# Two attention layers of a graph network run as one loop of units

## The chip, the core and the metric

The kernel runs on one core of one Trainium2 chip. The metric is the device time of one execution in microseconds. A core has TensorE (PE, matmuls; its weight loads are shown as PEld), VectorE (DVE), ScalarE (ACT), GpSimd (POOL, which issues the gathers here) and SyncE (SP, which issues the plain transfers). Each engine works through its own queue in order; semaphores tie the queues together.

## What is computed

Four graph layers follow each other on 3327 nodes with 512 features: a graph attention (layer 0), a neighbourhood mean with linear maps (layer 1, the "sage" stage), and two more attentions (layers 2 and 3). Each takes `h = relu(layernorm(x))` and adds its result to `x`. The two layers that the change touches have one form:

```python
hp = jnp.einsum('nd,hdf->hnf', h, W)              # 8 heads of 64 features
f_src = jnp.einsum('hnf,hf->hn', hp, a_src)
f_dst = jnp.einsum('hnf,hf->hn', hp, a_dst)
e = jax.nn.leaky_relu(f_src[:, :, None] + f_dst[:, None, :], ALPHA)
e = jnp.where(adj[None] > 0, e, NEG_FILL)
att = jax.nn.softmax(e, axis=-1)
out = jnp.einsum('hij,hjf->hif', att, hp)
out = jax.nn.elu(jnp.transpose(out, (1, 0, 2)).reshape(N, H * F))
```

The graph is sparse, and its nodes are sorted so that the first ones have far more neighbours than the last.

## The kernel before

Nodes are padded to 3328: 26 blocks of 128 rows, or 52 groups of 64 target nodes. An attention reads a table in HBM with one row of 528 words for each source node: eight heads of 64 features of `h W`, each with an exponential beside it, and eight more exponentials. `PLAN` gives each group three counts: dense blocks (128 table rows that lie together, brought by SP), mixed and pure rows sets (128 table rows each, picked by an index list and gathered by POOL). Group 0 has (14, 5, 4), group 1 (6, 4, 6), the last ones about (1, 1, 3). There are 77 dense blocks and 291 gathers in one attention.

Blocks are taken in the order 0, 24, 1, 23, 2, 22, ..., 11, 13, 12, 25 (`ls.order`), each with its two groups. `Lists.units` cuts a group's rows into units: dense and mixed ones in units of up to 2 (`SLOTS`), then pure ones in units of up to 3 (`UNIT`).

`attend` runs over the units; PE, DVE and ACT keep the order in which it is written there. A dense or mixed unit costs VectorE two operations, `mx` (L1553, a maximum of the group's row `r_bc` and the table's exponentials) and `wgt` (L1557, times the mask), and TensorE 32 small matmuls into the group's sum `facc` (L1588). An edge unit (pure rows) costs TensorE a pick `r_of` (L1487), VectorE a sum `w_of` (L1495), a maximum (L1540) and a product `vw` (L1543), and TensorE matmuls into `facc` (L1577). The pick for a unit stands two units ahead in TensorE's order. The row `r_bc` of a group is fetched by SP (`r_two`, L1343) and spread over the partitions by a matmul (L1351). Rows are loaded three units ahead (`AHEAD`), by `take` (L1309 on SP, L1314 on POOL).

At the end of a unit `later` moves everything that runs beside: the endings of groups (`ending`: `sums`, reciprocal, eight scalings into `fhp`, L1404; then `elu_into`, `fin_e` and `fin_x`), and one tick of the next layer's projection. In attention 2 that is `Following` for layer 3. For each finished block of `x3` it normalises (`norm`, on ScalarE), transposes (`p_ps`, L961), forms `p_sd` (L969) and `p_wh` (L980, eight matmul passes of 512 columns for `h W`), scales it into the table row on ScalarE (L989), writes the row to table 3 (L990) and the other values to `r_dram`. One step of it is done in each tick, for at most two blocks, the second starting five ticks after the first (`lag`). When the units of attention 2 are used up, `hurry` hands the projection spare PSUM banks and it goes on with normalisation (`norm_by_columns`, L879 to L888) and scaling (L984) on VectorE. Only when it has ended does the second call of `attend` begin, for attention 3.

The call that the change replaces, and the loop at the end of `attend`:

```python
over.append(True)
if beside is not None:
    mx = aps.tile([P, SLOTS, BANK], F32, name="mx", tag="mx", bufs=1)
    rb = aps.tile([P, BANK], F32, name="r_bc", tag="r_bc", bufs=1)
    beside.hurry((mx[:, 0, :], mx[:, 1, :], rb))
while ends or (beside is not None and beside.busy()):
    later()
```

Of the kernel before, what the change touches and what calls it, by code (L numbers as in the profile page):

```python
# [39 lines left out]
P = 128  # L40
H = 8
# [31 lines left out]
AHEAD = 3  # L73
EPARTS = 5
# [465 lines left out]
class Lists:  # L540
# [46 lines left out]
    def units(self, g):  # L587

        dense, mixed, pure = PLAN[g]
        rows, out = self.rows(g), []  # L590
        for edge, part, most in ((False, rows[: dense + mixed], SLOTS), (True, rows[dense + mixed :], UNIT)):
            n, at = -(-len(part) // most), 0
            for b in range(n):
                w = len(part) // n + (b < len(part) % n)
                out.append((edge, part[at : at + w], self.edge[g] + at))
                at += w
        return out
# [209 lines left out]

class Following:
# [3 lines left out]
    def __init__(self, tc, cs, N, wl, W, WA, table, r_dram, r3, pool, psum, pb, lag, ab=None):  # L812

        self.__dict__.update(locals())
        nc = tc.nc
        if ab is not None:
            self.ab = pool.tile([P, 2, D], F32, name=f"ab{wl}")
            for k, a in enumerate(ab):
                nc.sync.dma_start(self.ab[:, k, :], a.partition_broadcast(P))
        self.NB = table.shape[0] // P  # L820
        self.Wt = pool.tile([P, KC, D], F32, name=f"fWt{wl}")
        nc.sync.dma_start(self.Wt, W.rearrange("(kc p) o -> p kc o", p=P))
        self.hs = pool.tile([P, self.NB, KC], F32, name=f"hs{wl}")
        self.early, self.ready, self.spare, self.taken, self.gone = [], [], None, {}, []

    def begin(self, c, xt):
        self.early.append((self.norm_by_columns if self.spare is not None or self.ab is not None else self.norm)(c, xt))
# [4 lines left out]
    def hurry(self, spare):  # L832

        self.spare = spare

    def bank(self, shape, name, k):
        if self.spare is not None:
            return self.spare[k][: shape[0], : shape[1]]
        return self.psum.tile(shape, F32, name=name, tag="p_ps", bufs=self.pb)

    def tick(self):
        if self.spare is not None:
            for g in self.ready[:2]:
                if next(g) is None:
                    self.ready.remove(g)
            self.step()
            return
        if self.lag:
            for n, g in enumerate(self.ready[:2]):
                if n and self.taken[id(self.ready[0])] < self.lag:  # L850
                    break
                self.taken[id(g)] = self.taken.get(id(g), 0) + 1
                if next(g) is None:
                    self.gone.append(g)
            while self.gone:
                g = self.gone.pop()
                self.ready.remove(g)
                del self.taken[id(g)]
            self.step()
            return  # L860
# [96 lines left out]
    def rest(self, c, hx):  # L957
# [9 lines left out]
        sd = self.bank([P, BANK], "p_sd", 0)  # L967
# [10 lines left out]
        wh = self.bank([P, D], "p_wh", 1)  # L978
        for kc in range(KC):
            nc.tensor.matmul(wh, hT[:, kc, :], self.Wt[:, kc, :], start=(kc == 0), stop=(kc == KC - 1))  # L980
        yield True
        nc.vector.tensor_scalar(sf, sf, -SMALL, SMALL, ALU.max, ALU.min)
        if self.spare is not None:
            nc.vector.tensor_tensor(  # L984
                V[:, :, 0:F], wh.rearrange("p (h f) -> p h f", f=F), V[:, :, F : F + 1].to_broadcast([P, H, F]), ALU.mult
            )
        else:
            for h in range(H):
                nc.scalar.mul(V[:, h, 0:F], wh[:, h * F : (h + 1) * F], V[:, h, F : F + 1])  # L989
        nc.sync.dma_start(self.table[c * P : (c + 1) * P, :ROW], row.bitcast(I32))  # L990
        rs = halves(nc, pp, self.cs, sf, self.r3[:, c, :])
        if self.spare is None:
            yield True
        yield True
        rs, last = rs()
        if self.spare is None:
            yield True
        yield True
        tr = self.bank([2 * H, P], "p_tr", 2)
# [277 lines left out]
def sparse(ctx: ExitStack, tc: tile.TileContext, t: dict, out: bass.AP, WA, ls, cs, idx, rdeg, first):  # L1277
# [41 lines left out]
    def attend(layer, table, r_dram, r3, finish, tick=lambda: None, home=None, beside=None, edges=None):  # L1319
# [5 lines left out]
        width = table.shape[1]  # L1325
        groups = [b * PG + u for b in ls.order for u in range(PG)]
        units = []
        for j, g in enumerate(groups):
            mine = ls.units(g)
            spread_at = sum(not e for e, _, _ in mine) - 1  # L1330
            units += [(j, g, e, rows, s0, i == 0, i == len(mine) - 1, i == spread_at) for i, (e, rows, s0) in enumerate(mine)]
        hq = H // PG
        sw = hq * (F + 1)
        with tc.tile_pool(name=f"fatt{layer}", bufs=2) as ap, tc.tile_pool(
# [5 lines left out]
            def fetch(j):  # L1340
                if j < len(groups):
                    rr = ap.tile([2, H * GB], F32, name="r_two", tag="r_two", bufs=2)
                    nc.sync.dma_start(rr, r_dram[groups[j], :, :, :].rearrange("t h i -> t (h i)"))  # L1343
                    rrs[j] = rr

            def spread(j):


                if j < len(groups):
# [4 lines left out]
            def ending(g, hps={}, made={}):  # L1354

                b, u = divmod(g, PG)
                o0 = u * GB
                fin = finish(b, lambda: hps.pop(b), ap)

                def place():  # L1360

                    if b not in hps and home is None:
                        hp_ = hps[b] = ap.tile([P, D], F32, name="fhp", tag="hp", bufs=3)
                    elif b not in hps:
                        hps[b] = home[:, b, :]
                    return hps[b]
# [4 lines left out]
                if over:  # L1371
                    sm = accs.pop(g)[:, :sw].rearrange("p (q x) -> p q x", x=F + 1)
# [11 lines left out]
                    made[b] = made.get(b, 0) + 1  # L1384
                    if u == PG - 1:
                        while made[b] < PG:
# [4 lines left out]
                nc.scalar.copy(sm, accs.pop(g)[:, :sw])  # L1391
                sm = sm.rearrange("p (q x) -> p q x", x=F + 1)
                yield
                if layer == 2:
# [10 lines left out]
                made[b] = made.get(b, 0) + 1  # L1405
# [4 lines left out]
            def later():  # L1410
# [3 lines left out]
                tick()  # L1414

            def load(i):

                if i < len(units):
                    _, _, e, rows, _, _, _, _ = units[i]
                    if e:  # L1420
                        gi = ap.tile([P, UNIT, width], I32, name="rows_e", tag="rows_e", bufs=5 if layer == 0 else 6)
                    else:
                        gi = ap.tile([P, SLOTS, width], I32, name="rows_s", tag="rows_s", bufs=4 if layer == 0 else 5)
                    loaded[i] = gi
                    take(gi, table, rows)

            def bits(i):

                if layer == 0 and i < len(units):
                    _, g, _, rows, _, _, _, _ = units[i]  # L1430
# [10 lines left out]
            def masks(i, on):  # L1441

                if i < len(units):
                    _, _, e, rows, _, _, _, _ = units[i]
# [12 lines left out]
            def turned(i):  # L1457

                if layer == 0 and i < len(units) and units[i][2]:
                    _, g, _, rows, _, _, _, _ = units[i]  # L1460
# [6 lines left out]
            def kept(i):  # L1467

                if layer == 0 and i < len(units) and units[i][2]:
                    _, g, _, rows, s0, _, _, _ = units[i]  # L1470
# [7 lines left out]
            def pick(i):  # L1478

                if i < len(units) and units[i][2]:  # L1480
                    _, g, _, rows, s0, _, _, _ = units[i]
# [4 lines left out]
                    for k in range(len(rows)):  # L1486
                        nc.tensor.matmul(re[:, k, :], st[:, k, :], r3[mine, b, :], start=True, stop=True)  # L1487

            def summed(i):

                if i < len(units) and units[i][2]:
                    n, re = len(units[i][3]), found.pop(i)
# [3 lines left out]

            for j in range(2):
# [4 lines left out]
            lead = [(ahead + 1 if layer == 0 else 2) if u[2] else 1 for u in units]  # L1502
# [29 lines left out]
            for i, (j, g, e, rows, s0, begins, stops, last_slots) in enumerate(units):  # L1532
                n, m0 = len(rows), rows[0][0]
                gt = loaded.pop(i).bitcast(F32)
# [24 lines left out]
                early(i)  # L1559
                if begins:  # L1560
                    fetch(j + 2)
                    acc = aps.tile([P, BANK], F32, name="facc", tag="acc")
                    accs[g] = acc
# [6 lines left out]
                for k in range(n):  # L1570
# [3 lines left out]
                    if e:  # L1574
                        by = vw[:, k].rearrange("p (q v) x -> p v q x", v=PG)
                        for v in range(PG):
                            nc.tensor.matmul(  # L1577
                                accs[g][v * GB : (v + 1) * GB, :sw].rearrange("p (q x) -> p q x", x=F + 1),
# [6 lines left out]
                    for q in range(hq):  # L1585
                        for v in range(PG):
                            h = q * PG + v
                            nc.tensor.matmul(  # L1588
                                accs[g][v * GB : (v + 1) * GB, q * (F + 1) : (q + 1) * (F + 1)],
# [10 lines left out]
                later()  # L1600
                if stops:
                    ends.append(ending(g))
            over.append(True)
            if beside is not None:
                mx = aps.tile([P, SLOTS, BANK], F32, name="mx", tag="mx", bufs=1)
                rb = aps.tile([P, BANK], F32, name="r_bc", tag="r_bc", bufs=1)
                beside.hurry((mx[:, 0, :], mx[:, 1, :], rb))
            while ends or (beside is not None and beside.busy()):
# [37 lines left out]
    with ExitStack() as mx:  # L1646
# [85 lines left out]
        with tc.tile_pool(name="beside_ps", bufs=1, space=PSUM) as wps:  # L1732
# [8 lines left out]
            attend(0, *first, done, lambda: next(bg, None), y)  # L1741
# [135 lines left out]
    with ExitStack() as l3:  # L1877
        at2 = proj
        proj = following(l3, 3, 2, t["L3_gnn_W"], 2, 5)
        attend(2, at2.table, at2.r_dram, at2.r3, elu_into(x2, x3, proj.begin), proj.tick, beside=proj, edges=edges)  # L1880
    attend(3, proj.table, proj.r_dram, proj.r3, elu_into(x3, out), edges=edges)
# [101 lines left out]
```

## Time and profile before

| what | value |
|---|---|
| median of 3 timed runs | 2659.47 us (2657.05 to 2659.57) |
| the profiled execution | 2389.36 us, its span 2387.6 us |
| mean TensorE clock granted in it | 0.87 |
| busy over the span: PE, DVE, ACT, POOL | 1868.2, 1706.4, 1110.2, 1162.9 us |
| gathers `rows_e`, `rows_s` of the three attentions | 654 and 219, 957 and 964 ns each |
| `p_wh`, `fhp` scalings | from 3.70 us a block, 334 ns each |

Stages by the trace, in us from the start of the span: lists and first projection to about 352, attention 0 to about 860, sage and the projection of layer 2 to 1394, attention 2 to about 1910, the end of its endings and of the projection of layer 3 to 1944, attention 3 to the end. The profiled execution is 270 us shorter than the timed ones; durations below are those of the profiled one. Busy times of PE are modelled, since matmuls overlap.

### The profile page before, as it was taken

The numbers are of one execution on the slowest core, as the hardware profiler recorded it, in microseconds if no ns is written. First come the engines' busy times: TensorE is split into PE (matmuls) and PEld (weight loads), VectorE is DVE, ScalarE is ACT, GpSimd is POOL, SyncE is SP. The second block draws the span as 40 slices with busy tenths as digits, with TensorE's granted clock in tenths as the row PEclk, the third lists the DMA queues.
The fourth block names the chain that finished last, engine by engine and source line by source line (L and its number), as shares of the span: only waits on it lengthen the run. The fifth ranks groups of instructions, "written<-read, shape, count | busy, mean of one in ns | idle before, by whom it ended". The sixth has DMA issues, their size and how long they took to land. (4 is left out here: it accounts for less than half of the span.)

```text
span 2387.6 us, 43165 instructions
## 1 busy us (share of the span) xinstructions
PE 1868.2 (78%) x14899; PEld 1042.4 (44%) x14899; DVE 1706.4 (71%) x3061; ACT 1110.2 (47%) x4149; POOL 1162.9 (49%) x1227
## 2 busy tenths in 40 slices
PE   5888416897888869899999936888888857776875
PEld 4554204454555424333333324555444435444442
DVE  5455866788989895044445549878787749999996
ACT  3566101455666633133333312577796822445543
POOL 1000013476777500477776435655655335776762
PEclk9887757899999979999999968888898966779777
DMA  6676118798889665689888688877787548888883
GB/s 274 245 291 225 42 39 299 264 316 287 270 261 295 197 247 189 216 280 307 292 287 296 219 248 272 246 246 227 235 253 223 155 182 260 271 278 259 278 287 118
DMA packets 213728, 577.63 MB, mean 242 GB/s; under 512 B 37838, under 2 KB 44076, under 8 KB 210174
## 3 DMA queue, kind: packets, MB, share of 16 engines
q0 software_dynamic: 93504, 328.25, 43.6%
q1 hardware_dynamic: 119998, 246.53, 29.8%
q8 instruction: 121, 1.98, 0.3%
q14 instruction: 105, 0.86, 0.1%
HBM read 511.41 MB, written 63.25 MB: 241 GB/s over the span
## 5 line engine op out<-in xcount | busy, mean ns | idle before, releaser
L1314 POOL DMA_INDIRECT rows_e<-table,idx x654 | 625.9, 957 | 363.0 <-issue 148.3
L1577 PE MATMUL facc<-vw,ones_of 128*64 128x260 f32 x2616 | 447.2, 457 | 78.5 <-DVE vw L1543 61.0
L1588 PE MATMUL facc<-rows_s,wgt 128*64 128x65 f32 x7200 | 343.9, 247 | 170.8 <-DVE wgt L1557 115.8
L1588 PEld LDWEIGHTS facc<-rows_s,wgt 128*64 128x64 f32 x7200 | 289.8, 156 | 291.2 <-DVE wgt L1557 147.7
L1543 DVE TENSOR_TENSOR vw<-rows_e,w_of 128x1040 f32<-128x1040 f32 (+1 forms) x270 | 395.6, 1465 | 9.6 <-DVE w_of L1540 0.2
L1314 POOL DMA_INDIRECT z_rows<-h_dram,idx x291 | 278.8, 958 | 237.0 <-issue 156.3
L1314 POOL DMA_INDIRECT rows_s<-table,idx x219 | 211.1, 964 | 239.1 <-PE facc L1588 142.9
L1553 DVE TENSOR_TENSOR mx<-r_bc,rows_s 128x1024 f32<-128x1024 f32 (+1 forms) x255 | 280.4, 1100 | 46.6 <-DMA rows_s<-table 34.1
L1557 DVE TENSOR_TENSOR wgt<-mx,mask 128x1024 f32<-128x1024 f32 (+1 forms) x255 | 280.3, 1099 | 38.4 <-ACT mask L1455 20.9
L1404 ACT ACTIVATE fhp<-sums,rd 64x64 f32<-64x64 f32 x816 | 215.6, 334 | 185.3 <-DVE rd L1397 182.1
L1577 PEld LDWEIGHTS facc<-vw,ones_of 128*64 128x64 f32 x2616 | 195.4, 156 | 225.7 <-issue 94.2
L1867 PE MATMUL sage_acc<-z_rows,z_mask 128*64 128x512 f32 x736 | 188.7, 611 | 11.5 <-DMA z_rows<-h_dram 5.9
L1218 POOL DMA_DIRECT2D list_b<-shift x8 | 4.0, 513 | 325.3 <-DVE shift L1179 325.3
L1820 DVE TENSOR_TENSOR s_o<-n_ps,bn_y 128x512 f32<-128x512 f32 x26 | 18.0, 692 | 150.2 <-PE n_ps L1815 141.8
L1851 ACT CAST z_mask<-mask 128x128 f32<-128x128 uint8 (+1 forms) x201 | 52.5, 284 | 154.4 <-PE sage_acc L1867 154.0
L741 PE MATMUL wh_ps<-fWt,hT 128*128 128x512 f32 x208 | 121.5, 738 | 0.0
L1391 ACT COPY sums<-facc 128x260 f32<-128x260 f32 x153 | 56.1, 367 | 140.5 <-PE facc L1577 139.3
L1404 ACT ACTIVATE bn_y<-sums,rd 64x64 f32<-64x64 f32 x408 | 107.7, 334 | 2.9 <-DVE rd L1397 1.3
L1495 DVE TENSOR_REDUCE w_of<-r_of 128x16 f32<-128x48 f32 (+1 forms) x270 | 61.4, 227 | 62.1 <-PE r_of L1487 35.9
L1867 PEld LDWEIGHTS sage_acc<-z_rows,z_mask 128*64 128x64 f32 x736 | 51.4, 137 | 114.8 <-issue 94.0
L1789 PE MATMUL s_ps<-fWx,hT 128*128 128x512 f32 x208 | 93.9, 605 | 5.1 <-ACT hT L1786 5.1
L1455 ACT ACTIVATE mask<-on 128x128 uint8<-128x128 uint16 (+1 forms) x85 | 25.2, 297 | 153.3 <-DVE on L1433 151.0
(260 smaller groups left out, 3006.8 us busy)
## 6 DMA issues: line engine op xcount, KB each, us to landing
adj_i<-in_adj SPq DMA_DIRECT2D x26, 1664.0 KB
rows_s<-table SPq DMA_DIRECT2D x46, 528.0 KB
table<-v_row SPq DMA_DIRECT2D x78, 264.0 KB
rows_s<-table SPq DMA_DIRECT2D x62, 264.0 KB
rows_s<-table SPq DMA_DIRECT2D x23, 632.0 KB
fin_x<-fx SPq DMA_DIRECT2D x52, 256.0 KB
z_rows<-h_dram SPq DMA_DIRECT2D x23, 512.0 KB
rows_e<-table,idx POOLq DMA_INDIRECT x654
```

The source lines that it names most:

```text
L741: nc.tensor.matmul(wh, hT[:, kc, :], self.Wt[:, kc, :], start=(kc == 0), stop=(kc == KC - 1))
L1314: nc.gpsimd.indirect_dma_start(out=dst, out_offset=None, in_=src[:, :], in_offset=bass.IndirectOffsetOnAxis(ap=idx[:, k : k + 1], axis=0))
L1391: nc.scalar.copy(sm, accs.pop(g)[:, :sw])
L1404: nc.scalar.mul(hp[o0 : o0 + GB, h * F : (h + 1) * F], sm[mine, q, 0:F], rd[mine, q, :])
L1495: nc.vector.tensor_reduce(w[:, :n], re[:, :n].rearrange("p k (t h) -> p k h t", h=H), AX.X, ALU.add)
L1543: nc.vector.tensor_tensor(vw[:, :n], gt[:, :n, : H * (F + 1)].rearrange("p k (h x) -> p k h x", x=F + 1), w[:, :n].unsqueeze(3).to_broadca ...
L1553: nc.vector.tensor_tensor(mx[:, :n], rbs[j].unsqueeze(1).to_broadcast(full), T.unsqueeze(3).to_broadcast(full), ALU.max)
L1557: nc.vector.tensor_tensor(wt[:, :n], mx[:, :n], mk.unsqueeze(2).to_broadcast(full), ALU.mult)
L1577: nc.tensor.matmul(accs[g][v * GB : (v + 1) * GB, :sw].rearrange("p (q x) -> p q x", x=F + 1), ones_of[i][:, k, :], by[:, v], start=f, stop=l,
L1588: nc.tensor.matmul(accs[g][v * GB : (v + 1) * GB, q * (F + 1) : (q + 1) * (F + 1)], wt[:, k, h, :], gt[:, k, h * (F + 1) : (h + 1) * (F + 1)],
L1789: nc.tensor.matmul(ps, hT[:, kc, :], Wx[:, 0, kc, :], start=(kc == 0), stop=(kc == KC - 1))
L1867: nc.tensor.matmul(acc[u * GB : (u + 1) * GB, :], m, z, start=f, stop=l)
```

## The change

Attentions 2 and 3 become one call of `attend` with two `Stage` objects, and its units one list. The second stage begins with the dense blocks of its first two groups, at most `HEAD` = 10 of each (10 of group 0, 6 of group 1, so eight units), out of order of the groups; then the groups follow as before, without those blocks. A unit of stage 1 may be loaded once its rows are in the table: dense blocks when each has been projected (`done`), gathers when stage 0 has `drained`. Until then each unit calls `later` three times (`HASTE`). `hurry` is gone: the projection's last blocks are done as all the others are, and the last endings of attention 2 too. `p_wh` is issued in two halves of four passes, one tick apart, and the scaling follows a tick later than before.

```diff
+HEAD = 10
+HASTE = 3
...
-    def units(self, g):
+    def units(self, g, skip=0):
...
-        for edge, part, most in ((False, rows[: dense + mixed], SLOTS), (True, rows[dense + mixed :], UNIT)):
+        for edge, part, most in ((False, rows[skip : dense + mixed], SLOTS), (True, rows[dense + mixed :], UNIT)):
...
+class Stage:
+    def __init__(self, table, r_dram, r3, finish, tick=None, home=None, beside=None):
+        self.__dict__.update(locals())
...
     def tick(self):
-        if self.spare is not None:
-            for g in self.ready[:2]:
-                if next(g) is None:
-                    self.ready.remove(g)
-            self.step()
-            return
-        if self.lag:
-            for n, g in enumerate(self.ready[:2]):
+        for n, g in enumerate(self.ready[:2]):
...
-        wh = self.bank([P, D], "p_wh", 1)
+        wh = self.bank([P, D], "p_wh")
         for kc in range(KC):
             nc.tensor.matmul(wh, hT[:, kc, :], self.Wt[:, kc, :], start=(kc == 0), stop=(kc == KC - 1))
+            if kc % 2:
+                yield True
+        nc.vector.tensor_scalar(sf, sf, -SMALL, SMALL, ALU.max, ALU.min)
+        for h in range(H):
+            nc.scalar.mul(V[:, h, 0:F], wh[:, h * F : (h + 1) * F], V[:, h, F : F + 1])
+        nc.sync.dma_start(self.table[c * P : (c + 1) * P, :ROW], row.bitcast(I32))
+        self.done.add(c)
+        rs = halves(nc, pp, self.cs, sf, self.r3[:, c, :])
         yield True
...
-    def attend(layer, table, r_dram, r3, finish, tick=lambda: None, home=None, beside=None, edges=None):
+    def attend(layer, stages, edges=None):
...
+        for z, st in enumerate(stages):
+            groups = [b * PG + u for b in ls.order for u in range(PG)]
+            seq, head = [], HEAD if z else 0
+            for g in groups[:PG]:
+                d = min(head, PLAN[g][0])
+                seq += [(g, False, ls.rows(g)[k : min(k + SLOTS, d)], None) for k in range(0, d, SLOTS)]
+            for g in groups:
+                d = min(head, PLAN[g][0]) if g in groups[:PG] else 0
+                seq += [(g, *u) for u in ls.units(g, d)]
...
+            def drained(z):
+                return z == 0 or (reached[0] == z and not ends and not stages[z - 1].beside.busy())
+
             def load(i):
                 if i < len(units):
...
+                    waiting.append(i)
+                while waiting:
+                    _, z, _, _, rows, _, _, _, _, _ = units[waiting[0]]
+                    if not drained(z) and not all(d and c in stages[z - 1].beside.done for _, d, c in rows):
+                        return
+                    bring(waiting.pop(0))
...
+                reached[0] = z
+                while i not in loaded:
+                    later()
+                    load(len(units))
...
-                later()
+                for _ in range(1 if drained(z) else HASTE):
+                    later()
...
-            if beside is not None:
-                mx = aps.tile([P, SLOTS, BANK], F32, name="mx", tag="mx", bufs=1)
-                rb = aps.tile([P, BANK], F32, name="r_bc", tag="r_bc", bufs=1)
-                beside.hurry((mx[:, 0, :], mx[:, 1, :], rb))
-            while ends or (beside is not None and beside.busy()):
+            while ends:
                 later()
...
-        attend(2, at2.table, at2.r_dram, at2.r3, elu_into(x2, x3, proj.begin), proj.tick, beside=proj, edges=edges)
-    attend(3, proj.table, proj.r_dram, proj.r3, elu_into(x3, out), edges=edges)
+        second = Stage(at2.table, at2.r_dram, at2.r3, elu_into(x2, x3, proj.begin), proj.tick, None, proj)
+        attend(2, [second, Stage(proj.table, proj.r_dram, proj.r3, elu_into(x3, out))], edges)
```

## The prediction

> **What bounds the kernel now.** I read the split of the span into stages first (busy time by stretch), then the order of time around the passage from attention 2 to attention 3, then who waits for whom inside the two attentions. The chain of waits at the end covers only the last 3 us and says nothing about this place.
>
> Busy time by stretch (from:to, length, then busy us and instruction count of each engine, PE clock, DMA share, GB/s): attention 2, the passage, attention 3.
>
> ```profile
> 1394.00:1910.00 516.00, 412.44 (x4028) 247.47 (x4029) 406.33 (x706) 336.76 (x1358) 280.39 (x291) 0.86 0.77 237
> 1910.00:1944.00 34.00, 22.10 (x62) 11.14 (x60) 10.53 (x34) 11.84 (x66) 0.00 (x0) 0.77 0.11 40
> 1944.00:2388.00 444.00, 313.14 (x3542) 200.58 (x3542) 392.06 (x546) 177.39 (x601) 280.01 (x291) 0.77 0.80 257
> ```
>
> Columns three to seven are PE, PEld, DVE, ACT, POOL. Attention 3 is a VectorE stage (392 of 444 us), attention 2 is shared by VectorE (406 of 516) and TensorE (412), and in the passage nothing is full: no gather runs and the DMA engines are at 0.11.
>
> The passage in order of time (start, length, engine, line; in brackets the idle time before and what ended it):
>
> ```profile
> 1900.64 1.78 DVE L1543 TENSOR_TENSOR vw<-rows_e,w_of 128x1560 f32<-128x1560 f32 x1
> ...
> 1915.22 5.34 PE L980 MATMUL mx<-fWt,hT 128*128 128x512 f32 x8 [2.44 <-ACT s_col L976]
> ...
> 1925.95 5.10 PE L980 MATMUL mx<-fWt,hT 128*128 128x512 f32 x8 [0.48 <-ACT s_col L976]
> ...
> 1934.90 5.40 PE L980 MATMUL mx<-fWt,hT 128*128 128x512 f32 x8 [0.48 <-ACT s_col L976]
> ...
> 1941.14 0.38 SPq L990 DMA_DIRECT2D table<-v_row  x1
> ...
> 1944.49 0.94 POOL L1314 DMA_INDIRECT rows_e<-table,idx  x1 [61.02 <-DMA r_two<-r_dram]
> ...
> 1947.97 1.23 DVE L1553 TENSOR_TENSOR mx<-r_bc,rows_s 128x1024 f32<-128x1024 f32 x1 [6.12 <-DMA rows_s<-table]
> ```
>
> The last product of attention 2 ends at 1902.42, the last block of table 3 is written from 1941.14, the first gather starts at 1944.49 (42.1 us after that product), and VectorE's first operation of attention 3 at 1947.97: 45.5 us in which the engine that bounds both sides does only small work. Three projections, one after another, make up most of it. Then, between 1947.97 and 1980, VectorE is busy 24.2 of 32 us: idle 7.8.
>
> Who waited for whom in the passage and the start of attention 3 (us in total, times, longest), and VectorE's longest waits in attention 2:
>
> ```profile
> DVE v_row L984 <- PE mx L980: 14.3, 3, 5.1
> DVE mx L1553 <- DMA rows_s<-table: 10.6, 5, 6.1
> ...
> DVE w_of L1495 <- PE r_of L1487: 32.9, 18, 5.5
> DVE r_half L797 <- ACT r_half L793: 9.2, 5, 2.9
> ```
>
> The first two show the projections and then the dense loads, which start together with 16 gathers at a DMA share above 1. The third is the largest wait of VectorE inside attention 2: in order of time 13 of the 18 (29.3 us) come right behind a `p_wh` block, 3.70 us of TensorE in one piece (26 of them).
>
> [...]
>
> **The change part by part.**
>
> *Head units.* Sixteen dense blocks (10 of group 0, 6 of group 1) become 8 units that run before the table is whole. A unit is two VectorE operations, 1.23 + 1.22 us, spaced 2.53 us (1947.97 to 1950.50): 8 x 2.53 = 20.2 us leave the time behind the first gather. Loads of them go out while the DMA engines are at 0.11, so the 7.8 us of starvation go. Two more dense units (blocks 10 to 13 of group 0) need no gather and stand right behind the head, 5.1 us; they cover the 3.5 us from first gather to first operation. Sum of what can go: 20.2 + 7.8 + 3.5 = 31.5 us.
>
> *Price of the new order behind it.* The gathers now have less dense work beside them. Groups 0 and 1 need 19 gathers; POOL does one per 1.25 us (0.95 and 0.30 gap), so 23.8, and with about 2.5 of landing (estimate from the 3.5 just named) and the last unit's 2.5 it is 28.8 us. VectorE needs for the same stretch 5.1 (two dense units) + 6.4 + 3.7 (group 0: 5 mixed, 4 edge rows) + 5.1 + 5.0 (group 1: 4 and 6) + 0.3 = 25.6. Stall 3.2, bounds 0 and 8. Over all of attention 3 POOL needs 291 x 1.25 = 364 us against nearly 400 of VectorE, so it doesn't become the bound. Between head and rest the row `r_bc` (one buffer) is spread anew with no edge unit between to hide it: 2 us (dense matmuls 1.0 and 0.8 for the spread, at the low clock), once; the other such place lies inside the drain.
>
> *The drain.* It now goes in ticks, three per unit, normalises on ScalarE again, and TensorE has a dense unit between its steps. By the order of the changed program, TensorE works in the first five head units: dense matmuls 5 x 2.0 (low clock); three `p_ps` 0.66 to 1.12; three round trips through `hT` of 1.3; three `p_sd` 1.04 to 1.89; three `p_wh` 3.70 to 5.43; two transposes and a spread, 1.1. Sum 31 to 40.5 us from 1905.2, when TensorE ends attention 2. With 1.74 for the scaling and some queueing the last table write comes at 1939 to 1948, against 1941.1. I take 1944, d = +3; bounds -2 and +7. ScalarE has 17 us of work in 1905 to 1945 now; it gets one ending (2.5), two normalisations (6.2 more than the logarithm and exponential it has now) and three scalings (5.2): about 31 of 40, so it fits, but little idle time is left. VectorE loses 5.8 of its 12.1 there (summed over stretches of 5 us) and gains 20.2: 26.5 of 40. POOL has nothing to do until the table is whole. On SP, loads of head units wait for their blocks of the table, which are old by then (block 9 is projected as the 19th of 26), and for a `rows_s` buffer, with table writes queued behind them; that buffer is freed by a dense unit which stands ahead of the `p_wh` in question on TensorE, so nothing is delayed.
>
> So this part gives 31.5 - 3.2 - 2 - 3 = 23.3 us.
>
> *h W in halves.* Nothing is added on TensorE; a block takes one tick more, which at a lag of 5 (9 ticks, two in flight) doesn't lower the rate. Each wait behind a `p_wh` can lose one half, 1.85 us, or all of itself if shorter: over the 13 waits and one of 3.95 us on `r_bc` that is 22.5 us at most. The second half then stands in the next unit, and TensorE is busy about 87% there (349 of 400 us in 1500 to 1900), so much comes back. I take 9 us; bounds -5 (two interruptions for one) and +20.
>
> Other edits (`hurry` and its spare banks gone, stages as objects, two more row fetches of 4 KB) cost nothing outside the drain counted above.
>
> **Profile and median.** In the profiled execution (2389.36 us, span 2387.6) the sum is 23.3 + 9 = 32, so 2357. The timed runs are 270 us longer, median 2659.47. The trace can't show where; if TensorE's clock is lower there (the stage between the attentions had 508 of 534 us busy at 0.99), attention 2 hangs on TensorE more and the halves bring less: I take 5. The first part is idle time of VectorE and I carry it over unscaled. 2659.5 - 23.3 - 5 = 2631.
>
> **Rivals.**
> 1. As worked out, 2631: 0.58.
> 2. Drain at full clock, halves pay nearly in full: 31.5 - 2 - 0 + 2 = 31.5 and 19: 2609. For: 29 us of waits directly behind `p_wh`. Against: TensorE at 87%. 0.15.
> 3. The drain in ticks is longer (d = +15, because ScalarE, VectorE and TensorE queue in step): 11 from the first part, 1 from the second: 2647. For: ScalarE was busy 32 of 35 us in 1880 to 1915. 0.14.
> 4. The gathers take over as the bound: 291 of them follow a start that doesn't move. At 1.45 us each under contention they need 422 us, and 429 are there now: about 2655. Against: 1.25 spacing even at a DMA share above 1. 0.06.
> 5. Slower: three ticks in each head unit run strictly in series with it, the unit's matmuls waiting for VectorE, VectorE for ScalarE's small results, ScalarE for TensorE. The last table write falls in unit 7, so at 6 us a unit (42/7) it is as now; the point is 9.8 us a unit (31.5 - 5.2 = 26.3 more over 7). At 11 it costs 35 and the kernel is 9 slower: 2668. 0.07.
>
> **Numbers.** Faster by over 0.2% (5.3 us, about what a measurement here can tell from no change): rivals 1 to 3, 0.87; same: 4, 0.06; slower: 0.07. Range 2608 to 2652: it covers 1 and 3 and the near side of 2, and leaves out the far side of 2, 4 and 5.
>
> **What would show it.** In the profile after: VectorE's `mx` and `wgt` of table 3 between about 1903 and 1940 at 5 to 6 us spacing; the last table write within 38 to 46 us of the last product of attention 2; POOL starting 3 us later; a VectorE wait on gathers of some 3 us in the next 30; the wait on `r_of` in attention 2 down from 33 to about 20. Wrong it would be if the spacing is 9 us or more, if VectorE waits on gathers far into attention 3, or if attention 2 itself gets longer.

## The result and the profile after

The changed kernel takes 2690.01 us (median of four runs, 2683.19 to 2700.83) against 2658.26 (2650.70 to 2659.57) for the kernel before: a ratio of 1.0129, 95% interval 1.0086 to 1.0172. It is 31.8 us slower where 28 faster were forecast.

The sets of runs below are of two kinds: in one ("quick") the kernel before takes 2377 to 2381 us, in the other ("slower") 2658 to 2691. What makes the kind is not shown: the texts below speak of quick and slower chips, but the record gives the same chip number, 9, for a quick set (the fourth) and a slower one (the fifth). The result and its profile (span 2693.0 us, clock 0.824) belong to the slower kind, the profile of before shown above to the quick kind, so the two can't be subtracted stage by stage. Here, therefore, is the busy time by stretch of the changed kernel (attention 2, passage, rest of attention 3; columns as above):

```profile
1550.00:2102.00 552.00, 438.57 (x3987) 258.98 (x3988) 405.23 (x694) 328.52 (x1323) 276.30 (x288) 0.83 0.73 222
2102.00:2156.00 54.00, 38.40 (x300) 23.70 (x300) 24.34 (x51) 33.13 (x142) 0.48 (x1) 0.78 0.33 106
2156.00:2690.00 534.00, 346.55 (x3351) 212.79 (x3349) 378.41 (x532) 181.52 (x602) 276.41 (x291) 0.68 0.68 201
```

and beside it that of a kernel on the slower kind whose only edit is one empty tick in a block of the projection, and which took 1.0021 of the time of before (`b_delay` below):

```profile
1555.00:2115.00 560.00, 446.49 (x3994) 268.99 (x3995) 404.61 (x694) 332.63 (x1328) 276.55 (x288) 0.82 0.70 215
2115.00:2157.00 42.00, 26.15 (x95) 13.41 (x93) 12.91 (x47) 19.43 (x94) 0.00 (x0) 0.78 0.11 40
2157.00:2680.00 523.00, 341.61 (x3542) 213.65 (x3542) 392.02 (x546) 179.05 (x600) 280.36 (x291) 0.73 0.70 218
```

The move itself took place: 24.3 us of VectorE in the passage instead of 12.9, and 378 instead of 392 behind it. But the passage is 54 us instead of 42, and the rest of attention 3 takes 534 us instead of 523 with 14 us less VectorE work in it. In order of time the passage of the changed kernel looks so (start, length, engine, line, idle time before):

```profile
2100.61 1.78 DVE L1568 TENSOR_TENSOR vw<-rows_e,w_of 128x1560 f32<-128x1560 f32 x1
...
2105.53 1.23 DVE L1578 TENSOR_TENSOR mx<-r_bc,rows_s 128x1024 f32<-128x1024 f32 x1
...
2122.00 1.23 DVE L1578 TENSOR_TENSOR mx<-r_bc,rows_s 128x1024 f32<-128x1024 f32 x1
...
2133.44 1.23 DVE L1578 TENSOR_TENSOR mx<-r_bc,rows_s 128x1024 f32<-128x1024 f32 x1
...
2142.41 0.33 DVE L760 TENSOR_REDUCE hm<-hs 128x4 f32<-128x104 f32 x1 [6.41 <-ACT hT L960]
...
2152.61 0.32 SPq L982 DMA_DIRECT2D table<-v_row  x1
2153.03 0.17 DVE L799 TENSOR_TENSOR r_half<-r_full,r_half 128x8 fp32r<-128x8 f32 x1 [7.32 <-ACT r_half L795]
...
2155.52 0.94 POOL L1305 DMA_INDIRECT rows_s<-table,idx  x1 [81.85 <-DMA table<-v_row]
```

Seven head units start from 2105.53 to 2153.22, on average 7.9 us apart. VectorE stands before small results of ScalarE (6.41, 7.32 us) with the next dense unit behind it in order. The last block of the table is written 50.2 us after the last product of attention 2 (2102.39).

VectorE's waits in the rest of attention 3 (us in total, times, longest; "issue" is idle time for which the profile shows no releaser), the changed kernel:

```profile
DVE fin_x L1657 <- ACT fin_x L1653: 20.1, 15, 1.8
DVE w_of L1515 <- PE facc L1614: 19.7, 12, 8.4
DVE rd L1402 <- ACT sums L1396: 18.2, 12, 5.8
...
DVE rd L1402 <- issue: 10.3, 13, 1.1
...
DVE fin_x L1657 <- issue: 9.4, 7, 1.6
```

and `b_delay`, of the same kind, in the same stretch:

```profile
DVE fin_x L1636 <- ACT fin_x L1632: 2.5, 2, 1.4
...
DVE rd L1399 <- ACT sums L1393: 0.7, 1, 0.7
```

Two operations of VectorE, `rd` and `fin_x`, both steps of a group's *ending*, now wait: 38 us for ScalarE and 20 without a releaser, 58 us in 47 waits where there were 3, far behind the passage. Nothing in the forecast spoke of them.

### The profile page after: what moved, and what is told of

Its sections match the earlier page's. It is cut to its first block, busy times and chain, and to the rows that moved or that the text cites. A ratio compares the mean times of both kernels' runs of the same rounds, so it can differ in the third digit from the quotient of the medians.

```text
span 2693.0 us, 43173 instructions
## 1 busy us (share of the span) xinstructions
PE 1997.6 (74%) x14901; PEld 1103.8 (41%) x14901; DVE 1699.0 (63%) x3050; ACT 1128.5 (42%) x4196; POOL 1158.2 (43%) x1227
## 3 DMA queue, kind: packets, MB, share of 16 engines
q8 instruction: 121, 1.98, 0.3%
## 5 line engine op out<-in xcount | busy, mean ns | idle before, releaser
L1603 PE MATMUL facc<-vw,ones_of 128*64 128x260 f32 x2616 | 498.9, 492 | 147.5 <-DVE vw L1568 90.3
L1614 PE MATMUL facc<-rows_s,wgt 128*64 128x65 f32 x7200 | 388.3, 255 | 189.7 <-issue 115.0
L1614 PEld LDWEIGHTS facc<-rows_s,wgt 128*64 128x64 f32 x7200 | 320.6, 163 | 334.5 <-issue 209.9
L1603 PEld LDWEIGHTS facc<-vw,ones_of 128*64 128x64 f32 x2616 | 214.3, 168 | 326.6 <-issue 199.4
L1838 PE MATMUL n_ps<-fWx,aT 128*128 128x512 f32 x208 | 101.4, 632 | 23.0 <-issue 19.2
L976 PE MATMUL p_wh<-fWt,hT 128*128 128x512 f32 x208 | 116.5, 690 | 0.7 <-ACT v_row L970 0.7
L1494 ACT CAST edges<-st_ps 64x384 bf16<-64x384 f32 (+1 forms) x90 | 37.0, 411 | 162.4 <-PE st_ps L1485 85.2
```

Source lines behind the costliest of these rows:

```text
L1603: nc.tensor.matmul(accs[z, g][v * GB : (v + 1) * GB, :sw].rearrange("p (q x) -> p q x", x=F + 1), ones_of[i][:, k, :], by[:, v], start=f, ...
L1614: nc.tensor.matmul(accs[z, g][v * GB : (v + 1) * GB, q * (F + 1) : (q + 1) * (F + 1)], wt[:, k, h, :], gt[:, k, h * (F + 1) : (h + 1) * (F ...
L1838: nc.tensor.matmul(ps, aT[:, kc, :], Wx[:, 1, kc, :], start=(kc == 0), stop=(kc == KC - 1))
```

## The experiments

**Where it is lost.** `drained` is a gate that was meant to open once, when attention 2 is through. As written it asks that no ending is open, and `ends` holds those of attention 3 too. So it closes again each time a group of attention 3 stops, and while it is closed each unit moves the endings three steps (`HASTE`) and no gather is written out; a unit whose rows aren't loaded moves further steps until all endings are through. Followed through the program as written, 102 of the 175 units of attention 3 make three steps (7 of them in the drain), and at 7 places two more steps are forced. One edit lets the gate stay open:

```diff
 def drained(z):
-    return z == 0 or (reached[0] == z and not ends and not stages[z - 1].beside.busy())
+    if z and reached[0] == z and not ends and not stages[z - 1].beside.busy():
+        opened.add(z)
+    return z == 0 or z in opened
```

`a_latch` has it. `a_whole` keeps the gate as it is and puts h W in one piece:

```diff
-            if kc % 2:
+            if kc == KC - 1:
                 yield True
```

`b_halves` is the kernel before with the halves alone (its edit is shown further down), `b_again` the kernel before.

> The kernel before, unchanged, for a profile of an ordinary execution (about 2658 us) to set beside that of the changed one (2693 us): the profile shown at first was of an execution of 2389 us. If the loss lies in the last attention, its stage here is about 500 us against the 534 us of the changed kernel and the stages up to the end of attention 2 agree within 5 us. If the halves of h W cost it, attention 2 is some 30 us shorter here than the 567 us of the changed kernel. If the passage costs it, that stretch here is no longer than the 44 us there.

> The changed kernel, with the gate made to stay open once it has opened (edit: the first time that attention 3 is reached with no ending open and the projection done, this is remembered). Theory A, the gate: as written it closes again whenever a group of attention 3 has an ending open, so that each unit then moves the endings three steps instead of one and VectorE stands before ScalarE's result; waits of VectorE for sums and fin_x in attention 3 were 18 and 20 us. It expects 2690 to fall by 30 to 45, to about 2650, with those two waits under 5 us together. Theory B, the halves of h W or the order of attention 2: no change, 2690. Theory C, the drain or the late gathers at the start of attention 3: no change, 2690.

> The changed kernel with h W in one piece of eight passes again and one tick less for a block. Theory A (the gate): the halves gained a few us, so this is 2690 to 2700. Theory B (the halves cost it, by moving the small steps behind them one unit later): 2655 to 2665. Theory C (drain and start): 2690.

> The kernel before with h W in two halves one tick apart (in one piece still when the projection is hurried at the end), nothing else changed. Theory A (the gate) and C: 2650 to 2658, the halves gain up to 8 us. Theory B (the halves): 2680 to 2690.

The set was of the quick kind (before 2377.33). `b_again` 1.0012 (0.9998 to 1.0025), so it gave no ordinary profile of the slower kind. `a_latch` 1.0069 (1.0041 to 1.0096), `a_whole` 1.0229 (1.0201 to 1.0258), `b_halves` 1.0087 (1.0056 to 1.0118). So neither theory alone holds: the halves cost about 21 us, and with the halves gone the changed kernel is still 54 us slower. The first theory had expected the halves to gain.

The next set had the changed kernel (`a_again`), both edits together (`a_latch_whole`), the kernel before with an empty tick behind the product (`b_delay`), and the open gate for the number of steps alone, while `load` still asks the closing one (`a_latch_ticks`):

```diff
+def latched(z):
+    if drained(z):
+        opened.add(z)
+    return z in opened
...
-                for _ in range(1 if drained(z) else HASTE):
+                for _ in range(1 if latched(z) else HASTE):
```

```diff
         yield True
+        if self.spare is None:
+            yield True
         nc.vector.tensor_scalar(sf, sf, -SMALL, SMALL, ALU.max, ALU.min)
```

> The changed kernel, unchanged, on the chip of the other runs of this call. From the runs before, on a chip where the kernel before took 2377 us (attention 2 longer by 15 with the halves, the passage shorter by 12, attention 3 longer by 54 to 58 with the closing gate) theory A expects 55 to 65 us more than before there (2436), or about 32 on a chip of the kind where it takes 2658. If the parts don't add, the loss is smaller.

> The changed kernel with the gate that stays open and h W in one piece, so only the one loop, the head units and the drain in ticks are left of the change. If the parts add: passage 12 us shorter, attentions 2 and 3 as before, so 8 to 15 us below the kernel before (ratio 0.994 to 0.997). If the passage gives nothing without the halves (each product then holds TensorE in one piece in the drain): ratio 1.000.

> The kernel before with h W in one piece and one empty tick behind it, so that the scaling and all steps after it come one unit later, as with the halves. If the shift of the small steps cost the 20 us of the halves, it is 15 to 20 us slower than before; if the split itself did (two interruptions of TensorE for one), it is within 3 us of before.

> The changed kernel where only the number of ticks in a unit is bound to the gate that stays open; loads of attention 3 still ask the gate that closes again. If the hurried endings are what costs, it equals the kernel with the whole gate latched (13 us above before on the quick chip, ratio 1.007). If it is the loads that are held back, it equals the changed kernel.

It was of the slower kind (before 2682.21): `a_again` 1.0112 (1.0069 to 1.0156), `a_latch_whole` 1.0007 (0.9982 to 1.0032), `b_delay` 1.0021 (1.0001 to 1.0042), `a_latch_ticks` 1.0276 (1.0238 to 1.0314). With gate and halves undone the whole loss is gone. `b_delay` lies between its two expectations. `a_latch_ticks` missed both of its expectations, and the miss explains the gate: with one step in a unit an ending stays open longer, the gate stays shut, and 120 steps are forced at 34 places just before a unit that needs its rows. Its waits of VectorE in attention 3:

```profile
DVE fin_x L1663 <- ACT fin_x L1659: 38.2, 15, 3.5
...
DVE rd L1402 <- ACT sums L1396: 10.5, 4, 2.6
```

So it isn't late gathers (VectorE waits for none in this stretch), nor three steps as such: it is every ending whose steps follow each other with no work of VectorE between them.

The third set (quick, before 2380.98) took up the kernel with both edits as `c_best`, and three variants of its drain: `HASTE = 5`, `HASTE = 2`, and `c_no_overlap`:

```diff
-                    if not drained(z) and not all(d and c in stages[z - 1].beside.done for _, d, c in rows):
+                    if not drained(z):
                         return
```

> The changed kernel with the gate that stays open and h W in one piece, a second time, since chips differ here: on one where the kernel before takes about 2680 us it was equal (ratio 1.0007). On a chip of the quick kind (2377) the parts measured there (passage 12 shorter, attention 2 as before, attention 3 up to 4 longer) give 8 to 12 below before, ratio 0.995 to 0.997. On a chip of the other kind again 0.998 to 1.003.

> The kernel of c_best with five steps in each unit of the drain instead of three, so that four dense units stand in the drain instead of seven. If the drain is a chain of small steps that hold VectorE and TensorE in order, whatever stands between, the last table write comes after about 46 us from the end of attention 2 instead of 50, but three dense units (7.5 us) fewer lie in it: 2 to 6 us slower than c_best. If the units between the steps delay the chain, the write comes at 40 and the gathers start 10 earlier: 3 to 8 faster.

> The kernel of c_best with two steps in each unit of the drain, so that ten dense units stand in it. If the units' own work (2.5 us of VectorE each) is hidden in the waits of the chain, the last table write comes within 3 us of c_best and the kernel is 2 to 6 faster; if each unit adds to the chain, the gathers start 8 or more later, and the kernel is 3 to 10 slower.

> The kernel of c_best where no row of attention 3 is loaded before the drain has ended, so that nothing of attention 3 runs beside it, and the drain goes in ticks one after another. It tells what the dense units beside the drain delay it by, and what they are worth. If the units delay the drain (11 us longer than before), the last table write here is at about 39 us from the end of attention 2, as in the kernel before; if the ticks themselves do (normalisation and scaling on ScalarE), it stays near 50. In time it is 20 to 30 us slower than c_best.

`c_best` 0.9932 (0.9915 to 0.9949): 14.6 us faster than before, a little more than the 8 to 12 expected. `c_haste5` 0.9966 (0.9954 to 0.9978), `c_haste2` 0.9956 (0.9939 to 0.9973), `c_no_overlap` 0.9980 (0.9968 to 0.9992). Five steps are slower than three; two can't be told from three, since the intervals overlap. Neither gained, though a gain was allowed for in both. The last table write hardly moves: it comes 48.2 us after the end of attention 2 with five steps, 50.2 with three, 49.3 with two. `c_no_overlap` is 9.7 us slower than `c_best`, where 20 to 30 were expected. `c_best` is the version to keep: it is below the kernel before on the quick kind, level with it on the slower one, and there 1% below the changed kernel. `c_best` and `a_whole` differ in the gate alone. The rest of attention 3 without and with the closing gate, `c_best` and then `a_whole`:

```profile
1942.00:2365.00 423.00, 292.85 (x3351) 184.63 (x3351) 375.33 (x534) 177.99 (x602) 280.01 (x291) 0.81 0.80 254
```

```profile
1943.00:2426.00 483.00, 320.55 (x3351) 198.51 (x3351) 378.76 (x534) 181.60 (x602) 277.43 (x291) 0.74 0.72 223
```

VectorE's work is equal (375 and 379), yet it takes 60 us more; TensorE's clock is lower too, 0.74 for 0.81. In `a_whole` VectorE's two waits are

```profile
DVE fin_x L1657 <- ACT fin_x L1653: 39.6, 26, 1.8
DVE rd L1402 <- ACT sums L1396: 18.8, 22, 1.1
```

58.4 us, and 2.5 and 0.6 us in `c_best`. In order of time in `a_whole`:

```profile
2108.28 1.23 DVE L1582 TENSOR_TENSOR wgt<-mx,mask 128x1024 f32<-128x1024 f32 x1
2110.61 0.18 DVE L1402 RECIPROCAL rd<-sums 128x4 f32<-128x4 f32 x1 [1.11 <-ACT sums L1396]
2110.72 1.23 DVE L1578 TENSOR_TENSOR mx<-r_bc,rows_s 128x1024 f32<-128x1024 f32 x1
2111.99 1.23 DVE L1582 TENSOR_TENSOR wgt<-mx,mask 128x1024 f32<-128x1024 f32 x1
2113.32 0.24 DVE L1515 TENSOR_REDUCE w_of<-r_of 128x24 f32<-128x72 f32 x1
2114.27 0.69 DVE L1657 SCALAR_TENSOR_TENSOR fin_x<-fhp,fin_x 128x512 f32<-128x512 f32 x1 [0.71 <-ACT fin_x L1653]
```

`rd` and `fin_x` stand in VectorE's queue before ScalarE has made their input, and everything behind them waits: 1.2 us on average, 48 times.

**Split or tick?** The fourth set (quick, before 2379.55) took the halves apart. `d_halves` and `d_delay` are `b_halves` and `b_delay`; `d_split` is `d_halves` with one empty tick fewer behind the table write, so that a block takes as many ticks as before; `d_latch` is `a_latch`.

```diff
             nc.tensor.matmul(wh, hT[:, kc, :], self.Wt[:, kc, :], start=(kc == 0), stop=(kc == KC - 1))
-        yield True
+            if kc == KC - 1 or (kc % 2 and self.spare is None):
+                yield True
```

and in `d_split` besides:

```diff
         rs = halves(nc, pp, self.cs, sf, self.r3[:, c, :])
-        if self.spare is None:
-            yield True
         yield True
```

> The kernel before with h W in two halves, a second time, beside the two that take the edit apart. On a quick chip (before near 2380) again 1.006 to 1.012. On a slower one (before near 2680), if the halves cost there as much as on the quick one, the same; if there TensorE's slower clock and idle time hide it, 0.999 to 1.004.

> The kernel before with h W in one piece and an empty tick behind it (ratio 1.002 on a slower chip). If the tick costs what the halves cost, it is equal to d_halves within 0.2%; if the split does, it is within 0.3% of before.

> The kernel before with h W in two halves, but with one empty tick fewer behind it, so that a block takes as many ticks as before. If the split costs, it is equal to d_halves within 0.3%; if the added tick does, it is within 0.3% of before. If VectorE now meets ScalarE's exponential a tick too early, both are surpassed.

> The changed kernel with the gate that stays open, h W in halves. On a quick chip 1.005 to 1.010 as before (1.0069). On a slower one, where the changed kernel stands at 1.011 to 1.013 and the one with both parts undone at 1.0007: if the gate carries the loss, 1.000 to 1.003; if the halves do, 1.008 to 1.012.

`d_halves` 1.0095 (1.0071 to 1.0119), `d_delay` 0.9995 (0.9978 to 1.0012), `d_split` 1.0097 (1.0074 to 1.0121), `d_latch` 1.0043 (1.0025 to 1.0060), just below what was expected. The split costs, the tick is free: `d_halves` and `d_delay` take equally many ticks and differ in the split alone. Attention 2 of `b_again`, `d_delay`, `d_halves` and `d_split`, one line each:

```profile
1408.00:1909.00 501.00, 408.80 (x3995) 246.28 (x3995) 404.55 (x697) 329.29 (x1330) 276.80 (x288) 0.86 0.77 240
```

```profile
1400.00:1893.00 493.00, 406.31 (x3995) 247.70 (x3995) 404.63 (x697) 330.04 (x1330) 275.24 (x287) 0.86 0.79 244
```

```profile
1402.00:1923.00 521.00, 432.28 (x3988) 258.56 (x3989) 405.96 (x696) 328.05 (x1324) 274.71 (x287) 0.81 0.74 231
```

```profile
1400.00:1922.00 522.00, 429.73 (x4007) 252.80 (x4007) 405.87 (x695) 329.20 (x1328) 275.12 (x288) 0.83 0.75 231
```

The granted clock goes from 0.86 to 0.81 and 0.83, and TensorE is busy 23 and 21 us longer with the same matmuls, not in `p_wh` alone: in `d_halves` `p_wh` takes 94.8 us for 88.1 and `facc` 264.2 for 252.6. The median product took 3.70 us in one piece, the median half takes 1.98. The wait that the halves were to shorten, VectorE's for `r_of` in attention 2, first in `b_again`, then in `d_halves`:

```profile
DVE w_of L1495 <- PE r_of L1487: 32.5, 18, 5.5
```

```profile
DVE w_of L1496 <- PE r_of L1488: 47.3, 32, 5.1
```

It became longer: nearly twice as many waits. In `d_split` that wait is 30.2 us, but VectorE waits for `r_half` 36.2 us instead of 9.2, and the stage is as long as in `d_halves`; so `d_split` by itself doesn't show what the split costs. What lowers the granted clock in the two stages with the halves, to 0.81 and 0.83, these runs don't show.

**The sum and the drain.** The last two:

> The changed kernel, unchanged. On a quick chip (before near 2380) the parts add up to: product in halves +24 (c_best to d_latch), gate +45 to +58, loop and head units -14: 55 to 68 slower, ratio 1.023 to 1.029. If the parts don't add, 1.013 or less. On a slower chip again 1.011 to 1.013.

> The kernel of c_best in which the projection, from the first unit of attention 3 on, again normalises and scales on VectorE and leaves out its two empty ticks, as the hurried form of the kernel before did (spare banks apart). If the dropped hurry is what lengthened the drain, the last table write comes about 40 to 45 us after the end of attention 2 instead of 50, and the kernel is 3 to 8 us faster than c_best (ratio to before 0.990 to 0.992 on a quick chip). If the dense units between the steps do it, the write stays at 48 to 51 and the ratio at 0.993.

In `e_fast`, from the first unit of attention 3 on:

```diff
-        for h in range(H):
-            nc.scalar.mul(V[:, h, 0:F], wh[:, h * F : (h + 1) * F], V[:, h, F : F + 1])
+        if self.fast:
+            nc.vector.tensor_tensor(V[:, :, 0:F], wh.rearrange("p (h f) -> p h f", f=F), V[:, :, F : F + 1].to_broadcast([P, H, F]), ALU.mult)
+        else:
+            for h in range(H):
+                nc.scalar.mul(V[:, h, 0:F], wh[:, h * F : (h + 1) * F], V[:, h, F : F + 1])
...
-        yield True
+        if not self.fast:
+            yield True
```

and `norm_by_columns` for blocks that begin then. The set was of the slower kind (before 2691.42): `e_after` 1.0105 (1.0069 to 1.0140), `e_fast` 0.9977 (0.9954 to 1.0000). The changed kernel was therefore never timed on the quick kind. `e_fast` is at best a little faster than before; beside `a_latch_whole` (1.0007, in another set) the intervals overlap. Its last table write comes 49.1 us after the last product of attention 2, 50.4 in `a_latch_whole`: the dropped VectorE form is not what makes the drain long.

From the timelines, in us: attention 2 (first to last operation of its units on VectorE); then from its end to the start of unit 26 of attention 3, which holds the passage and the first gathers; then from there to the start of its last unit.

| kernel | kind | attention 2 | passage to unit 26 | rest |
|---|---|---|---|---|
| `b_again` | quick | 500.8 | 114.0 | 348.7 |
| `c_best` | quick | 494.1 | 101.7 | 352.3 |
| `c_no_overlap` | quick | 496.8 | 113.3 | 348.6 |
| `a_whole` (gate) | quick | 497.4 | 107.3 | 406.9 |
| `d_latch` (halves) | quick | 515.5 | 102.7 | 351.8 |
| `b_delay` | slower | 560.5 | 126.5 | 416.5 |
| `a_latch_whole` | slower | 554.8 | 130.1 | 417.0 |
| changed | slower | 552.4 | 135.4 | 432.8 |
| `a_again` (changed) | slower | 562.6 | 136.1 | 434.2 |
| `e_after` (changed) | slower | 558.3 | 134.1 | 435.5 |

## Why the prediction was wrong

**The step that failed** is one line of it: "Other edits (...) cost nothing outside the drain counted above." The three steps of a unit were priced in the drain alone, as if `drained` opened once, and none of the five rivals has this cost. It closes again at every ending of attention 3, and VectorE then stands before the ending's steps: 58 us in the changed kernel, 58 in `a_whole`. On the quick kind this costs 54.6 us in the rest of attention 3 (406.9 against 352.3, `a_whole` beside `c_best`) and 5.6 more up to unit 26 (107.3 against 101.7). On the slower kind it is 17 in the rest (434 against 417 in `a_latch_whole`) and 5 to 6 up to unit 26 (135 and 136 against 130): some 22 of about 30 us lost. There `a_latch_whole` also has h W in one piece; that can't touch the rest of attention 3, where no product is left, but may have a part in the 5 to 6. Without gate and halves the kernel is level with before on the slower kind and 0.7% faster on the quick one.

**h W in halves**, forecast at 9 us gained in the profile (bounds -5 to +20) and 5 in the timed runs: the sign was wrong, 23 us lost on the quick kind (1.0095), far outside the bounds. It counted the waits behind a `p_wh` but held TensorE's own time constant ("Nothing is added on TensorE"); TensorE's busy time grew by 23 us. On the slower kind the stage shows no loss of that size (552 to 561 us in three profiles without the halves, 552 to 564 in four with them; clock 0.82 in `b_delay`, 0.83 in the changed kernel), nor does the product itself: summed over attention 2 it takes 97 to 104 us there in one piece and 98 to 103 in halves, against 85 to 88 and 94 to 97 on the quick kind. The halves weren't timed alone on the slower kind.

**The drain**: d = +3 (bounds -2 to +7) was too small. (The 2.0 us it took for the matmuls of a dense unit, "low clock", are those of the profile of before from 1950 to 1980 us, where the granted clock was 0.50.) The last write comes 50.2 us after the last product, 38.9 in `b_delay`: +11. Rival 3 had this mechanism, at +15. With nothing of attention 3 beside it (`c_no_overlap`) it is 47.2, in `c_best` 50.2 and in `b_again` 38.7. So 8.5 us come from the drain in ticks and 3 from the dense units. Not the ScalarE form (`e_fast`); that leaves the lag of five ticks between two blocks, the lost spare banks and the endings, which weren't separated. Rival 5's strict series of steps shows in part: 7.9 us a unit, forecast 5 to 6; its point of loss was 9.8.

**Head units and price**: the move (20.2 us) was right, its worth wasn't. On the quick kind passage to unit 26 is 12.3 us shorter (114.0 to 101.7), of which the later rest gives 3.6 back; 23.3 were forecast. The drain explains most of that: with 11 in place of 3 the forecast's own sum is 31.5 - 3.2 - 2 - 11 = 15. Of the 14.6 by which `c_best` beats before, the overlap as such is the 9.7 between it and `c_no_overlap`. On the slower kind it comes to nothing: in `a_latch_whole` the first twelve units are through 12.5 us sooner than in `b_delay` (72.4 against 84.8 us from the end of attention 2), and the next thirteen take 57.7 us instead of 41.6. The forecast's stall of at most 8 us for late gathers isn't the cause; what the trace shows of it stands in the last section, and its cause stays open.

**From profile to median**: "I carry it over unscaled" was the other weak step. Idle time of VectorE was worth its length where VectorE is the bound (392 of 442 us busy in attention 3 of `b_again`): 58 us of waits cost 60 there. It was worth less on the slower kind, where all engines have idle time (in `b_delay` VectorE is busy 392 of 523 us, TensorE 342): 58 us of waits cost some 22.

**Right** were that POOL isn't the bound (the 291 gathers start at a median of 1.25 us apart, and VectorE waits for none of them in the rest of attention 3 of the changed kernel), that the table's rows don't hold up the head units' loads (VectorE waits for no load in its passage), and that POOL starts late by the drain's delay (53.1 us after the last product, 42.3 in `b_delay`).

## What to carry to other kernels

A condition that opens a phase must be remembered once true; if it is asked anew and reads a list that the new phase fills itself, it closes again without an error, and costs time far from the place that was changed. Look for it by counting, as the program is written out, how often each branch is taken. Steps of a side job that wait for another engine belong one to a unit of the main work (58 us of waits against 3 here), and a product that TensorE does in one piece isn't free to cut (here it cost 23 us on the quick kind): compare the granted clock of the stage before and after (here 0.86, then 0.81 and 0.83).

## What was not expected of the hardware

On the slower kind the engines have idle time for which the profile shows no releaser. TensorE's largest such group over the whole span is, in `b_delay` and then in `b_again`, which lacks only the empty tick but is of the quick kind:

```profile
PE facc L1590 <- issue: 135.6, 177, 5.0
```

```profile
PE facc L1588 <- issue: 5.5, 9, 1.1
```

In the changed kernel, of the slower kind too, the group is 115.0 us. At the first units that need gathers it looks so there:

```profile
2176.34 0.45 PE L1614 MATMUL facc<-rows_s,wgt 128*64 128x65 f32 x2 [0.94 <-issue]
2177.74 0.53 PE L1614 MATMUL facc<-rows_s,wgt 128*64 128x65 f32 x4 [0.95 <-issue]
2178.47 0.17 PE L1507 MATMUL r_of<-r_three,edges 64*128 64x24 bf16 x1 [0.20 <-issue]
2179.20 0.17 PE L1507 MATMUL r_of<-r_three,edges 64*128 64x24 bf16 x1 [0.56 <-issue]
```

A few matmuls come every 1.4 us, and behind them VectorE's `w_of`, whose input is `r_of`, waits (the line of 19.7 us further up). The same place is slow in all six profiles of the one loop on this kind (from unit 13 to unit 17 it takes 22 to 30 us, 10 in `c_best`, 13 in `b_delay`); there the gain of the passage is lost. The last packet of a gather of attention 3 ends at a median of 3.7 to 3.8 us after the gather's start in four profiles of the slower kind, and 4.0 to 4.1 in `c_best` and `b_again`, so they aren't late. What holds TensorE back there was not found.
